# A state-space layer and an attention layer on one core: the kernel's beginning put in a written order, and the work of its first two steps rearranged

## The chip, the cores and the metric

The kernel runs on one core of a Trainium2 chip. The metric is the device time of one execution in microseconds (us). Engines are named as in the profile: PE is the matrix engine (PEld its weight loads), DVE the vector engine, ACT the scalar engine with its function tables, POOL the fourth engine, SP the engine that only issues transfers. ACT and POOL issue transfers too.

## The reference

The input `x` is 4 images (B) of 512 channels (C) and 64 x 64 positions (L = 4096), in float32. Two layers, each with a residual:

```python
x = x + L0(group_norm(x))     # layer norm, mamba on 4 chunks of 128 channels, skip,
                              # layer norm, 512 x 512 projection
x = x + L1(group_norm(x))     # linear attention with 8 heads, ReLU on q and k
```

Group norm has 32 groups of 16 channels and needs the statistics of the whole image. The mamba of layer 0, with 256 inner channels and 16 states, is

```python
xi, z = split(in_proj(x));  xc = silu(conv4(xi) + conv_b)
dt, Bs, Cs = split(x_proj(xc));  dt = softplus(dt_proj(dt) + b)
h = exp(dt * A) * h + (dt * xc) * B_t          # per channel and state, along L
y = sum_over_states(h * C_t) + xc * D_param
out = out_proj(y * silu(z))
```

## The kernel before, in words

An image is cut into 8 tiles of T = 512 positions. A step is one chunk of 128 channels of one tile of one image, so there are 4 x 8 x 4 = 128 steps (`steps`, line 1023). Each step has 16 slots; a slot makes two scans of 128 x 512 on DVE (line 755), where the 128 rows are 32 channels by 4 states.

**What a step needs.** `inputs` (line 593) makes in_proj and convolution together: four products with the shifted tile and the weights `w_cv` give `pc`, a fifth gives `pz`; `silu` (line 1064) follows on ACT. `mixers` (line 658) makes `pd` (x_proj), copies the part for dt to `dt` and sends the rows for B and C to DRAM (`b_rows`, `c_rows`); three bf16 copies and two "minus" products (`parts`) prepare C for the matrix engine. `time_banks` and `time_steps` make dt (`pt`, softplus). `to_rows` (line 640) multiplies dt by xc on POOL and writes both to DRAM (`d_rows`), and `spread` (line 649) reads them back as `d_all`, laid out for the scans: in four parts of two transfers of 256 KB. `b_row` and `c_tail` read B and C back, each row to 32 partitions (`b_all`, `c_sb`).

**A slot** (line 741): `drive` makes `bx` on POOL (line 737) from `d_all` and `b_all`, `decay` makes `dA` with exp on ACT (line 729) into one of three banks, the scan on DVE makes `h`; every second slot `product` (line 775) multiplies `h` by C on DVE, and `fold_states` sums over the states on PE into `y`. Then come gate, out_proj, skip, and for a whole tile `leave`: `layer_scale` (line 461), the projection with `w_pr` (`pp`), the residual, and the store of the tile for layer 1. Norm weights are folded into `w_pr`: it is scaled by `g_sb` (line 315), and its mean over the input channels is taken off (`pw_mean`, line 319, then line 321), the bias goes into `pb` (line 313).

**What sets the order.** The main loop (line 1114) stands under `tc.manual_schedule()`: each engine and queue gets its instructions in an order that follows the written one. Work between slots is put there by hand, by slot numbers, by `later`, and from four queues of generators (`ahead`, `late`, `rest`, `light`) with a credit for PE; the attention of an image runs in these gaps while the next image is in layer 0, and that of the last image after the loop. What stands ahead of the loop, lines 167 to 1112, is left to a scheduler, which may put instructions in another order than the written one. There `now[0]` is `None`, so `later`, `until` and `clear` don't hold anything back. Lines 1201 to 1210, after the loop, have `now[0] = None` too.

**The beginning.** `stats0` (line 810) loads the 8 tiles of image 0 on SP (line 148; three tile buffers, `TILES`) and takes `bn_stats` on DVE (line 816); `aggregate` (line 341) ends it. `stats_end` makes scale and offset per channel. `tile_norm(0, 0)` loads tile 0 again, into `xn` (line 506), applies them on ACT (`group_norm`, line 374), and makes the layer norm: sums over channels on PE, `mu_sums` and `mu`, subtraction on DVE (line 435), squares on ACT (line 443), `var_sums` and `var`, Ln and Exp on ACT, multiplication on DVE (line 421), scale and bias on ACT (line 454). Lines 1091 to 1112 then prepare steps 0 and 1. Meanwhile ACT's queue loads all weights (lines 229 to 285): `w_x`, `conv_bc`, `w_z`, `w_xp` in five pieces, `w_dt`, the columns `dtb`, `dpar`, `g_sb`, `b_sb` (four bytes for each partition and column), `a_sb`, `w_op`, `sk`, `w_pr`, `pb`, `w_qk`, four rows of `b_qk`, `bv`, `bo`. Their preparation stands on DVE: `w_cv` (line 234), `dg` (264), `bqk` (287 to 291), `a_k` (296), the centring of `w_pr`. `a_t` comes from `a_k` with 16 small transfers on SP (line 300).

**Counters of transfers.** In the built program the transfers of SP and ACT share eight completion counters in turn. A transfer waits, before it is issued, for the one eight before it to have landed, whatever queue that one is on.

Of the kernel before, what the change touches and what calls it, by code (L numbers as in the profile page):

```python
# [14 lines left out]
P = 128  # L15
# [9 lines left out]
def kernel(  # L25
# [138 lines left out]
        return load(cols(x, b)[:, :, t * T : (t + 1) * T], f"x{why}_{b}_{t}")  # L164


    ident = wk.tile([P, P], F32, tag="sq", name="ident", bufs=4)
    make_identity(nc, ident)

# [55 lines left out]
    def const_rows(v, name):  # L225
        return rows(v, const.tile([P, v.shape[0] // P, v.shape[1]], F32, tag=name, name=name))
# [4 lines left out]
    nc.scalar.dma_start(w_x, in_w[:, 0:DI])  # L231
    conv_bc = wk.tile([P, NTAP, DI], F32, tag="h", name="conv_bc", bufs=2)
    nc.scalar.dma_start(conv_bc, conv_w.partition_broadcast(P))
    nc.vector.tensor_tensor(w_cv, conv_bc, w_x.unsqueeze(1).to_broadcast([P, NTAP, DI]), ALU.mult)
    w_z = const.tile([P, DI], F32, tag="w_z", name="w_z")
    nc.scalar.dma_start(w_z, in_w[:, DI : 2 * DI])
    cb = column(conv_b, NH, "cb")
# [22 lines left out]
    dpar = column(d_par, NH, "dpar")  # L260

    dg = const.tile([P, NH, BLK], F32, tag="dg", name="dg")
    for e in range(NH):
        nc.vector.tensor_scalar(dg[:, e, :], fold, dpar[:, e : e + 1], None, ALU.mult)
    g_sb = column(norm_g, NC, "g_sb")
    b_sb = column(norm_b, NC, "b_sb")
    skd = const.tile([P, BLK], F32, tag="skd", name="skd")
# [1 line left out]
    w_op = const_rows(op_w, "w_op")  # L269
    sk = const.tile([P, 1], F32, tag="sk", name="sk")  # L270
    nc.scalar.dma_start(sk, skip.partition_broadcast(P))
    w_pr = const_rows(proj_w, "w_pr")
    pb = column(proj_b, NC, "pb")
    w_qk = const_rows(wqk, "w_qk")


    bqk = const.tile([P, C], BF16, tag="bqk", name="bqk")
# [6 lines left out]
    bv = column(b_qkv[2 * C : 3 * C], NC, "bv")  # L284
    bo = column(b_out, NC, "bo")

    nc.vector.tensor_copy(bqk, b_qk)
    for i in (2, 3):
        r = slice(i * LANE, P)
        nc.vector.tensor_tensor(b_qk[r, :], b_qk[r, :], bqk[r, :], ALU.subtract)  # L290
        nc.vector.tensor_copy(bqk[r, :], b_qk[r, :])


    a_k = wk.tile([P, NH, KS, NQ], F32, tag="sq", name="a_k", bufs=4)
    nc.scalar.activation(a_k, a_sb.rearrange("p e (q k) -> p e k q", k=KS), AF.Exp)
    nc.vector.tensor_scalar(a_k, a_k, -1.0, None, ALU.mult)
    a_t = const.tile([P, NH, NJ, NQ], F32, tag="a_t", name="a_t")
    for k in range(KS):
        for j in range(NJ):
            nc.sync.dma_start(  # L300
                a_t[k * BLK : (k + 1) * BLK, :, j, :], a_k[j * BLK : (j + 1) * BLK, :, k, :]
            )
    nc.vector.tensor_scalar(skd, fold, sk, None, ALU.mult)


    for o in range(NC):
        pw = work_bank(f"pw_{o}")
        for c in range(NC):
            mm(
                pw[:, 0:1], w_pr[:, c, o * P : (o + 1) * P], b_sb[:, c : c + 1],  # L310
                start=(c == 0), stop=(c == NC - 1),
            )
        nc.vector.tensor_tensor(pb[:, o : o + 1], pb[:, o : o + 1], pw[:, 0:1], ALU.add)
    for c in range(NC):
        nc.vector.tensor_scalar(w_pr[:, c, :], w_pr[:, c, :], g_sb[:, c : c + 1], None, ALU.mult)

    pw = work_bank("pw_mean")
    for c in range(NC):
        mm(pw, ones.to_broadcast([P, P]), w_pr[:, c, :], start=(c == 0), stop=(c == NC - 1))
    for c in range(NC):  # L320
        nc.vector.scalar_tensor_tensor(
            w_pr[:, c, :], pw, -1.0 / C, w_pr[:, c, :], ALU.mult, ALU.add
        )
    pw = work_bank("pw_about")
    for c in range(NC):
        mm(
            pw[:, 0:1], ones.to_broadcast([P, P]), b_sb[:, c : c + 1],
            start=(c == 0), stop=(c == NC - 1),
        )
    about = const.tile([P, 1], F32, tag="about", name="about")  # L330
    nc.vector.scalar_tensor_tensor(about, pw[:, 0:1], -1.0 / C, sk, ALU.mult, ALU.mult)


    def stats_tile(name):
# [34 lines left out]
    def group_norm(dst, xt, norm):  # L369
        gr, off, _ = norm  # L370
        for c in range(NC):
            if c % 2 == 0:
                yield from clear()
            nc.scalar.activation(
                dst[:, c, :], xt[:, c, :], AF.Identity,
                bias=off[:, c : c + 1], scale=gr[:, c : c + 1],
            )
            if c == 1:
                yield "free"
        yield  # L380
# [12 lines left out]
    def mean_of(sums, what, when, stop=True):  # L393
# [13 lines left out]
        mm(bank, mean.to_broadcast([P, P]), got, start=True, stop=stop)  # L407
        return bank

    def over_deviation(v, var, name):  # L410
        rs = wk.tile([P, T], F32, tag="sq", name=f"rs_{name}", bufs=4)

        def root():
            nc.scalar.activation(rs, var, AF.Ln, bias=eps)
            nc.scalar.activation(var, rs, AF.Exp, scale=-0.5)

        rooted = later(1, root)
        yield
        yield from until(rooted)
        yield "wide"  # L420
        nc.vector.tensor_tensor(v, v, bc(var, NC), ALU.mult)  # L421
        free()
        norming.clear()
        yield

    def layer_norm(v, name):
        while norming:
            yield "wait"
        norming.append(name)
        yield from room()  # L430
        sums = work_bank(f"mu_sums_{name}")
        sums_into(sums, [v[:, c, :] for c in range(NC)], range(NC))
        mu = yield from mean_of(sums, f"mu_{name}", "one ahead")
        yield "wide"
        nc.vector.tensor_tensor(v, v, bc(mu, NC), ALU.subtract)
        free()
        yield "free"
        sqs = []
        for c in range(NC):
            if c % 2 == 0:  # L440
                yield from clear()
            sqs.append(wk.tile([P, T], F32, tag="sq", name=f"sq_{name}_{c}", bufs=4))
            nc.scalar.activation(sqs[c], v[:, c, :], AF.Square)
            if c == 1:
                yield "free"
        yield from room()
        sums = work_bank(f"var_sums_{name}")
        sums_into(sums, sqs, range(NC))
        var = yield from mean_of(sums, f"var_{name}", "two ahead")
        yield from over_deviation(v, var, name)  # L450
        for c in range(NC):
            if c % 2 == 0:
                yield from clear()
            nc.scalar.activation(
                v[:, c, :], v[:, c, :], AF.Identity,
                bias=b_sb[:, c : c + 1], scale=g_sb[:, c : c + 1],
            )
            if c % 2:
                yield "free"
# [43 lines left out]
    def normed(xn, pad, prev_pad, b, t, norm):  # L503

        body = xn[:, :, NTAP - 1 : NTAP - 1 + T]
        nc.sync.dma_start(body, cols(x, b)[:, :, t * T : (t + 1) * T])
        yield from pause(2)
        yield "free"
        if prev_pad is None:
            nc.gpsimd.memset(xn[:, :, 0 : NTAP - 1], 0.0)  # L510
        else:
            nc.gpsimd.tensor_copy(xn[:, :, 0 : NTAP - 1], prev_pad)
        yield from group_norm(body, body, norm)
        yield from layer_norm(body, f"a_{b}_{t}")
        nc.gpsimd.tensor_copy(pad, xn[:, :, T : T + NTAP - 1])
# [130 lines left out]
        f["d_rows", v] = d_rows  # L646
        later(1, lambda: nc.sync.dma_start(d_rows, both[:, v]))

    def spread(f, e, nm, part):

        if part == 0:
            f["d_all", e] = wk.tile([P, 2, NJ, T], F32, tag="d_all", name=f"d_all_{nm}_{e}")
        v, half = divmod(part, 2)
        src = f["d_rows", v].rearrange("(j i) e t -> i e j t", i=BLK)[:, e]
        for k in range(half * KS // 2, (half + 1) * KS // 2):
            nc.sync.dma_start(f["d_all", e][k * BLK : (k + 1) * BLK, v], src)

    def mixers(f, nm):

# [150 lines left out]
    def stats0(stats, b):  # L810

        for t in range(NT):
            xt = yield from load_x(b, t, "s")
            yield
            for c in range(NC):
                nc.vector.bn_stats(stats[:, c, t, :], xt[:, c, :])
                if c == NC - 1:
                    later(1, free_x)
                if c % 2:
                    yield "wait" if c == NC - 1 else None  # L820
# [214 lines left out]
    def input_norm(b):  # L1035
# [2 lines left out]
        norms[b] = yield from stats_end(aggregate(stats, f"a{b}"), f"a{b}")  # L1038
        yield

    def tile_norm(b, t):
        xn[b, t] = wk.tile([P, NC, NTAP - 1 + T], F32, tag="xn", name=f"xn_{b}_{t}", bufs=3)
        pads[b, t] = small.tile([P, NC, NTAP - 1], F32, tag="pad", name=f"pad_{b}_{t}")
        yield from normed(
            xn[b, t], pads[b, t], pads[b, t - 1] if t else None, b, t, norms[b]
        )
# [39 lines left out]
            queue.pop(0)  # L1086
        return False

    run(input_norm(0))
    run(tile_norm(0, 0))  # L1090
    run(step_inputs(0))
    silu(0)
    run(mixers(fs[0], names[0]))
    b_row(0)
    c_tail(0)
    time_banks(fs[0], names[0])
# [1 line left out]
    for v in range(2):  # L1098
        to_rows(fs[0], v, names[0])
    for part in range(4):  # L1100
        spread(fs[0], 0, names[0], part)
    for g in range(JJ, 3 * JJ, JJ):
        b_row(g)
    c_row(0)
    for g in range(2):
        drive(g)
    run(step_inputs(1))
    silu(1)
    run(mixers(fs[1], names[1]))
    nc.scalar.preload_act_table_set("natural_log_exp_and_others")  # L1110
    for k in range(LEAD):
        decay(k)

    with tc.manual_schedule():
        credit, seen, mix, held[0], held_x[0] = 0.0, work["mm"], iter(()), 0, 0
# [148 lines left out]
```

## Time and profile before

| | us |
|---|---|
| median of 3 runs | 7839.31 (7833.92 to 7841.01) |
| the profiled execution, its own time | 7841.1 |
| its span | 7839.4 |
| mean granted clock of PE | 0.905 of full |
| DVE idle in 140 to 7340 | 393.1 of 7200 |
| idle before the first tile's group norm on ACT | 16.34 |
| main loop's first scan starts | 120.77 |
| the last image's attention alone, after the last product (7363.67 + 1.76) | 7365.4 to the end |

The span is the time from first to last instruction in the profile, the execution's own time is 1.7 us longer. Busy times count each engine by itself; a low share is a loss only where no other engine is the bound. The page cuts the span into 40 slices of 196 us, so all of what the change touches at the beginning lies in the first one, and needs the trace's rows.

The early part of the trace, each with its start in us:

| what | start | note |
|---|---|---|
| the loads of the 8 tiles for the statistics, on SP | 0.80, 1.30, 11.96, 13.21, 21.52, 25.23, 35.35, 37.72 | the last lands at 45.2 |
| load of tile 0 into `xn` | 41.79 | |
| subtraction of the mean, L435 | 63.41 | 2.29 long, one 128x2048 |
| `pd` of step 0 | 91.24 | |
| softplus of step 0 | 96.44 and 98.88 | the second ends at 99.57 |
| `d_all` of step 0, 8 transfers | issued 102.92 to 106.6 | 7th landed at 114.5 |
| table load on ACT ahead of the first `dA` | 118.68 | 1.28 long |

### The profile page before, as it was taken

What the parts mean: (1) busy time and instruction counts of PE and PEld (TensorE: products, weight loads), DVE (VectorE), ACT (ScalarE), POOL (GpSimd) and SP (SyncE); (2) the same over time, 40 slices, a digit from 0 to 9 for tenths busy, and PEclk for the clock granted to TensorE, in tenths of its full rate; (3) what the DMA queues carried; (4) which work ended last, traced back from release to release, by engine and by line L of the source; (5) the groups of instructions that cost most, each with busy time, mean ns of one, the idle gap of its engine ahead of it and who ended that gap; (6) DMA issues with size and microseconds to landing.
All of it is one profiled execution on the core that took longest, in us unless ns stands there. A gap on an engine that the chain in (4) does not pass through costs nothing.

```text
span 7839.4 us, 90421 instructions
## 1 busy us (share of the span) xinstructions
PE 6444.4 (82%) x24839; PEld 2099.0 (27%) x24880; DVE 6905.7 (88%) x5650; ACT 5461.7 (70%) x8329; POOL 6898.4 (88%) x4649
## 2 busy tenths in 40 slices
PE   5677777677789888988788888898788888989599
PEld 1121212112223222322222223332222222323144
DVE  5999999999999999999999999999999999999500
ACT  4677777777777777777777777777777777777421
POOL 4999999999999999999999999999999999999500
PEclk7888878888899999998899999999899999999799
DMA  5666666666666656776666666676666666586302
GB/s 164 165 172 168 158 150 162 162 157 169 174 179 169 159 159 159 192 197 169 174 166 169 167 162 160 171 190 183 164 160 168 157 162 154 148 212 182 100 33 91
DMA packets 829184, 1265.87 MB, mean 161 GB/s; under 512 B 183912, under 2 KB 317560, under 8 KB 816384
## 3 DMA queue, kind: packets, MB, share of 16 engines
q1 hardware_dynamic: 804736, 1222.32, 59.6%
q0 software_dynamic: 16896, 33.56, 2.5%
q8 instruction: 195, 3.19, 0.2%
q10 hardware_dynamic: 7040, 4.20, 0.2%
q14 instruction: 317, 2.60, 0.1%
HBM read 1052.78 MB, written 206.57 MB: 161 GB/s over the span
## 4 chain that ended last, share of the span: by engine, by line
DVE 33%; PE 31%; ACT 10%; issue 8%; DMA 7%; POOL 7%; SPq 3%; POOLq 0%; DVEq 0%; ACTq 0%
DVE h L755 21%; DVE h L775 10%; PE pq L129 6%; PE y L129 6%; PE pc L129 5%; POOL bx L737 5%; ACT dA L729 4%; DMA d_all<-d_rows 3%; PE pr L129 3%; PE po L129 2%; SPq L704 2%; PE pp L129 2%; DMA c_sb<-c_rows 2%; PE pd L129 1%; DMA b_all<-b_rows 1%
## 5 line engine op out<-in xcount | busy, mean ns | idle before, releaser
L737 POOL TENSOR_TENSOR bx<-d_all,b_all 128x1024 f32<-128x1024 f32 x2048 | 4824.0, 2367 | 198.2 <-DVE h L755 178.6
L755 DVE TENSOR_TENSOR_SCAN h<-dA,st,bx 128x512 f32<-128x512 f32 x3584 | 4355.5, 1265 | 292.5 <-PE y L129 101.8
L729 ACT ACTIVATE dA<-d_all,a_t 128x512 f32<-128x512 f32 x4096 | 2759.0, 688 | 1491.5 <-DVE h L755 1434.8
L775 DVE TENSOR_TENSOR h<-h,c_all 128x1536 f32<-128x1536 f32 x1024 | 1768.6, 1727 | 0.1
L767 POOL TENSOR_TENSOR h<-h,c_sb 128x512 f32<-128x512 f32 x1024 | 1299.8, 1269 | 99.1 <-DMA c_sb<-c_rows 13.0
L129 PE MATMUL y<-h,fold 128*32 128x512 f32 x8192 | 1264.0, 693 | 45.7 <-POOL h L767 42.4
L129 PE MATMUL c_all<-parts,sel 128*128 128x384 bf16 x1024 | 369.4, 361 | 1021.9 <-DVE h L775 1020.7
L129 PE MATMUL pc<-xn,w_cv 128*128 128x512 f32 x2048 | 1036.6, 639 | 126.0 <-DVE xn L421 62.2
L129 PE MATMUL pq<-w_qk,xa 128*128 128x512 f32 x2048 | 962.5, 602 | 6.7 <-issue 4.1
L755 DVE TENSOR_TENSOR_SCAN h<-dA,bx 128x512 f32<-128x512 f32 x512 | 590.1, 1204 | 76.6 <-ACT dA L729 46.5
L129 PEld LDWEIGHTS pc<-xn,w_cv 128*128 128x128 f32 x2048 | 386.4, 199 | 735.6 <-issue 409.3
L129 PEld LDWEIGHTS <-sel 128*128 128x128 bf16 x1280 | 126.8, 99 | 1668.0 <-DVE h L775 1453.4
L129 PEld LDWEIGHTS pq<-w_qk,xa 128*128 128x128 f32 x2048 | 395.7, 195 | 437.4 <-issue 421.7
L129 PE MATMUL pp<-xn,w_pr 128*128 128x512 f32 x1024 | 478.0, 597 | 3.8 <-DVE xn L421 3.8
L129 PE MATMUL pr<-xb,m 128*128 128x512 f32 x1024 | 476.1, 603 | 4.8 <-POOL m L992 2.2
L129 PE MATMUL y<-xz,dg 32*32 32x512 f32 x2048 | 362.1, 785 | 0.0
L129 PEld LDWEIGHTS y<-h,fold 128*32 128x32 f32 x8192 | 170.5, 114 | 639.7 <-issue 398.1
L848 ACT ACTIVATE kq<-pq 128x512 f32<-128x512 f32 x256 | 150.8, 589 | 265.5 <-PE pq L129 264.8
L797 POOL TENSOR_TENSOR xz<-xz 128x512 f32<-128x512 f32 x256 | 325.1, 1270 | 10.2 <-ACT xz L794 9.3
L644 POOL TENSOR_TENSOR dt<-dt,xz 128x1024 f32<-128x1024 f32 x128 | 302.1, 2360 | 21.4 <-ACT dt L636 21.4
L855 DVE TENSOR_TENSOR kq<-pk,kq 128x256 f32<-128x256 f32 x124 | 51.2, 413 | 277.9 <-PE pk L129 277.7
L129 PE MATMUL pd<-xz,w_xp 128*128 128x512 f32 x512 | 289.3, 692 | 5.2 <-ACT xz L1066 5.2
(178 smaller groups left out, 6164.7 us busy)
## 6 DMA issues: line engine op xcount, KB each, us to landing
d_all<-d_rows SPq DMA_DIRECT2D x2048, 256.0 KB, 4.3
b_all<-b_rows SPq DMA_DIRECT2D x4096, 64.0 KB, 2.3
d_rows<-dt SPq DMA_DIRECT2D x256, 512.0 KB, 2.7
c_sb<-c_rows SPq DMA_DIRECT2D x4096, 16.0 KB, 3.5
xs<-in_x_dram SPq DMA_DIRECT2D x32, 1024.0 KB, 7.8
xn<-in_x_dram SPq DMA_DIRECT2D x32, 1024.0 KB, 8.4
xr<-in_x_dram POOLq DMA_DIRECT2D x32, 1024.0 KB, 10.2
x<-xr SPq DMA_DIRECT2D x32, 1024.0 KB, 4.5
```

The source lines that it names most:

```text
L129: nc.tensor.matmul(out_, lhsT, rhs, **how)
L644: nc.gpsimd.tensor_tensor(f["both"][:, 1], f["both"][:, 0], f["xz"][:, 0], ALU.mult)
L704: nc.sync.dma_start(dst[k * BLK : (k + 1) * BLK, :], rows_[q * KS + k, :].partition_broadcast(BLK))
L729: nc.scalar.activation(dAs[k], fs[n]["d_all", e][:, 0, j, :], AF.Exp, scale=a_t[:, e, j, q : q + 1])
L737: nc.gpsimd.tensor_tensor(bxs[g], fs[n]["d_all", e][:, 1, jj * 2 : jj * 2 + 2, :], bc(b_all[g // JJ], 2), ALU.mult)
L755: nc.vector.tensor_tensor_scan(h[:, j, :], dAs.pop(2 * g + i), bxs[g][:, i, :], 0.0 if t == 0 else st[:, c, e, q, j : j + 1], ALU.mult, AL ...
L767: nc.gpsimd.tensor_tensor(h[:, :, CUT:], h[:, :, CUT:], bc(c_sb.pop(g // JJ), NJ), ALU.mult)
L775: nc.vector.tensor_tensor(own, own, bc(c_all.pop(g // JJ), NJ), ALU.mult)
L797: nc.gpsimd.tensor_tensor(f["xz"][:, 1, e, :], f["xz"][:, 1, e, :], f["xz"][:, 0, e, :], ALU.mult)
L848: nc.scalar.activation(qk[i], pq, AF.Relu)
L855: nc.vector.tensor_tensor(kq, pk, kq, ALU.add)
```

## The change

The whole beginning is put under the manual schedule, so that its order on each engine follows the written one. (1) Tile 0 of `x` is loaded once, first of all, straight into `xn`; its statistics are taken there. (2) `w_pr` and `w_qk` leave ACT's queue: SP loads `w_pr` behind the last tile, `w_qk` behind the 16 transfers of `a_t`. (3) The preparation of the weights on DVE becomes functions called at tiles 2, 4 and 7. (4) Where `now[0]` is `None`, the two DVE operations of a norm (`over`) work in four blocks of 128x512 instead of one 128x2048, and `group_norm` puts chunks 1 and 3 on DVE; this holds after the loop too. (5) `spread` of step 0 comes in 16 transfers of 128 KB, those for the first slots ahead, instead of 8 of 256 KB. (6) The inputs of step 1 stand between the pieces of step 0; its `mixers` come behind the first three `dA`. (7) The offsets `pw`, the scaling and the centring of `w_pr` are spread over the beginning, the centring last; in the built program the four DVE instructions of the centring (line 321 before), though written ahead of the loop, stand between its third and fourth scan. (8) ACT's tables are loaded by written instructions: five before the loop, where there were six. The main loop's own code is unchanged.

```diff
+    front = ExitStack()
+    front.enter_context(tc.manual_schedule())
...
-    w_pr = const_rows(proj_w, "w_pr")
+    w_pr = const.tile([P, NC, C], F32, tag="w_pr", name="w_pr")
     pb = column(proj_b, NC, "pb")
-    w_qk = const_rows(wqk, "w_qk")
+    w_qk = const.tile([P, NC, 2 * C], F32, tag="w_qk", name="w_qk")
...
+    def offset_sums(o):
+        pw[o] = work_bank(f"pw_{o}")
         for c in range(NC):
             mm(
+                pw[o][:, 0:1], w_pr[:, c, o * P : (o + 1) * P], b_sb[:, c : c + 1],
                 start=(c == 0), stop=(c == NC - 1),
             )
...
+    def scaled():
+        for c in range(NC):
+            nc.vector.tensor_scalar(w_pr[:, c, :], w_pr[:, c, :], g_sb[:, c : c + 1], None, ALU.mult)
+
+    def centred():
+        pw = work_bank("pw_mean")
+        for c in range(NC):
+            mm(pw, ones.to_broadcast([P, P]), w_pr[:, c, :], start=(c == 0), stop=(c == NC - 1))
+        for c in range(NC):
+            nc.vector.scalar_tensor_tensor(
+                w_pr[:, c, :], pw, -1.0 / C, w_pr[:, c, :], ALU.mult, ALU.add
+            )
...
+            if now[0] is None and c % 2:
+                nc.vector.tensor_scalar(
+                    dst[:, c, :], xt[:, c, :], gr[:, c : c + 1], off[:, c : c + 1], ALU.mult, ALU.add
+                )
+            else:
+                nc.scalar.activation(
...
+    def over(v, m, op):
+
+        if now[0] is None:
+            for c in range(NC):
+                nc.vector.tensor_tensor(v[:, c, :], v[:, c, :], m, op)
+        else:
+            nc.vector.tensor_tensor(v, v, bc(m, NC), op)
...
-    def spread(f, e, nm, part):
+    def spread(f, e, nm, part, by_slot=False):
...
+        if by_slot:
+            half, v = divmod(part, 2)
+            ks, js = range(KS), slice(half * NJ // 2, (half + 1) * NJ // 2)
...
     def stats0(stats, b):
 
         for t in range(NT):
+            if (b, t) in xn:
+                for c in range(NC):
+                    nc.vector.bn_stats(stats[:, c, t, :], xn[b, t][:, c, NTAP - 1 :])
+                continue
             xt = yield from load_x(b, t, "s")
-            yield
+            yield t if now[0] is None else None
...
-    run(input_norm(0))
-    run(tile_norm(0, 0))
+    nc.scalar.preload_act_table_set("natural_log_exp_and_others")
+    new_xn(0, 0)
+    nc.sync.dma_start(xn[0, 0][:, :, NTAP - 1 :], cols(x, 0)[:, :, 0:T])
+    for t in input_norm(0):
+        if t == 2:
+            prepare_conv()
+        elif t == 4:
+            prepare_d()
+            prepare_bias()
+        elif t == NT - 1:
+            nc.sync.dma_start(w_pr, proj_w.rearrange("(c p) f -> p c f", p=P))
+            prepare_a()
+            nc.sync.dma_start(w_qk, wqk.rearrange("(c p) f -> p c f", p=P))
+    wide, taking = 0, []
+    for what in tile_norm(0, 0):
+        for o in taking:
+            offset_take(o)
+        taking = []
+        if what == "wide":
+            taking = ([0], [1, 2])[wide]
+            wide += 1
+            for o in taking:
+                offset_sums(o)
+    nc.scalar.preload_act_table_set("silu_and_others")
     run(step_inputs(0))
     silu(0)
-    run(mixers(fs[0], names[0]))
+    nc.scalar.preload_act_table_set("softplus")
+    second = step_inputs(1)
+    for _ in range(2):
+        next(second)
+    first = mixers(fs[0], names[0])
+    next(first)
+    next(first)
+    next(second)
     b_row(0)
     c_tail(0)
     time_banks(fs[0], names[0])
...
     for part in range(4):
-        spread(fs[0], 0, names[0], part)
+        spread(fs[0], 0, names[0], part, True)
+    nc.scalar.preload_act_table_set("silu_and_others")
+    run(second)
+    run(first)
+    c_row(0)
+    silu(1)
+    nc.scalar.preload_act_table_set("natural_log_exp_and_others")
     for g in range(JJ, 3 * JJ, JJ):
         b_row(g)
-    c_row(0)
     for g in range(2):
         drive(g)
-    run(step_inputs(1))
-    silu(1)
-    run(mixers(fs[1], names[1]))
-    nc.scalar.preload_act_table_set("natural_log_exp_and_others")
     for k in range(LEAD):
         decay(k)
+    offset_sums(3)
+    offset_take(3)
+    scaled()
+    run(mixers(fs[1], names[1]))
+    centred()
+    front.close()
```

## The prediction

> **What bounds the kernel now.** I read the page first, by engine and by slice.
>
> ```profile
> PE 6444.4 (82%) x24839; PEld 2099.0 (27%) x24880; DVE 6905.7 (88%) x5650; ACT 5461.7 (70%) x8329; POOL 6898.4 (88%) x4649
> DVE  5999999999999999999999999999999999999500
> ```
>
> Between a weak first slice and a weak end VectorE is above nine tenths in every slice. The windows view tells where the first slice is lost:
>
> ```profile
> 60.00:80.00 20.00, 11.03 (x21) 2.76 (x17) 4.58 (x2) 7.57 (x12) 0.19 (x1) 0.59 0.00 0
> 100.00:110.00 10.00, 9.97 (x21) 3.92 (x19) 0.00 (x0) 2.67 (x5) 1.98 (x1) 0.86 0.82 229
> 120.00:140.00 20.00, 11.85 (x37) 3.02 (x37) 18.08 (x15) 14.28 (x20) 18.99 (x13) 0.57 0.83 218
> 140.00:160.00 20.00, 13.55 (x59) 3.68 (x57) 20.00 (x17) 16.93 (x25) 19.76 (x14) 1.00 0.78 216
> ```
>
> Columns: window, length, busy time of PE, weight load, DVE, ACT, POOL, then clock, DMA share, GB/s. From 120 us DVE is the bound (1.92 us idle in 120–140, none in 140–200); before, the front is a chain. The main loop's order is the same in both builds on every engine, so a shift of the first product (L775) should reach the end unchanged. So I price the front up to that product, then the tail. The front's chain stands in the timeline:
>
> ```profile
> 51.78 1.04 DVE L341 BATCH_NORM_AGGREGATE mv_a<-st 128x2 f32<-128x48 f32 x4
> 56.68 2.93 ACT L374 ACTIVATE xn<-xn,off_a,gr_a 128x512 f32<-128x512 f32 x4 [16.34 <-DMA a_t<-a_k]
> 74.03 2.29 DVE L421 TENSOR_TENSOR xn<-xn,var_a 128x2048 f32<-128x2048 f32 x1 [8.33 <-ACT var_a L415]
> 77.22 9.70 PE L129 MATMUL pc<-xn,w_cv 128*128 128x512 f32 x16 [4.58 <-ACT xn L454]
> 99.59 2.77 SPq L647 DMA_DIRECT2D d_rows<-dt  x2
> 115.83 6.95 POOL L737 TENSOR_TENSOR bx<-d_all,b_all 128x1024 f32<-128x1024 f32 x3 [13.85 <-DMA b_all<-b_rows]
> 120.77 5.68 DVE L755 TENSOR_TENSOR_SCAN h<-dA,bx 128x512 f32<-128x512 f32 x5 [44.45 <-ACT dA L729]
> 126.37 1.73 DVE L775 TENSOR_TENSOR h<-h,c_all 128x1536 f32<-128x1536 f32 x1
> ```
>
> Start, busy time, engine, line; brackets hold the idle time and its releaser. The statistics end (S) at 52.82 (51.78 + 1.04), `pc` starts at 77.22, the first `bx` at 115.83, the first product at 126.37. I work out these four stretches: 52.82, 24.40, 38.61, 10.54.
>
> **1. Statistics: 52.82 → 42.0.** In SP's waits the tile loads are held by buffers and by other transfers:
>
> ```profile
> SPq L148 <- DVE st L816: 16.3, 4, 9.7
> SPq L148 <- DMA w_xp<-in_xp_w_dram: 10.1, 1, 10.1
> ```
>
> (Total, count, longest.) A load waits for the transfer eight earlier on its queue's counters. The change starts four tiles at once instead of three (with the weights some 5 MB at the 363 GB/s of window 5–10: the fourth lands at about 17.7), but puts new links in front of the rest. In the built order `dtb`'s issue on ACT waits for tile 3; `dpar`, `g_sb`, `b_sb`, `a_sb` follow, about 0.35 us each. `b_sb` is issued at about 19.5, and tile 5's load waits for it. The trace shows such column loads landing 4.8 to 9.0 us after issue (`dpar` 6.7, `b_sb` 9.0, both under six competing loads); I take 5.3, since only one tile then moves: 24.8. Tile 6 waits for `pb` in the same way, a little later. `b_qk`'s third and fourth rows wait for `a_sb` and tile 4 in the same way; the last lands at about 28; its five casts (0.41 + 0.69 + 0.42 + 0.69 + 0.42 = 2.63 by their rows) now stand on DVE ahead of tile 4's `bn_stats`, queued behind them: 30.7. Tile 4 takes 2.46 (the row of four 128x512): 33.1. That releases tile 7's load, which lands 4.8 later (5 to 7 have come): 38. Tiles 5 and 6 fill DVE to 38.1, `a_k` and `skd` 0.4, tile 7 2.46, L341 1.04: 42.0. Ends: 39 (casts ready early) and 46 (columns at 9.0). **−10.8.** Moved to SP behind tile 7, `w_pr` lands at about 40 and `w_qk` at about 55; `w_pr` is first read after the mean's "wide" block, at about 52, `w_qk` in the attention: cost nothing, with over 10 us of cover, and each us beyond it would cost one.
>
> **2. Norm: 24.40 → 21.1.** Two engines for L374: last block at +1.51 (two of .73) instead of +2.93: −1.4. [...] The row of L421 is 2.29 for 2048 columns; 512 columns take 0.69 alone, with a pitch of .615 in a row (2.46 for four): 2.54. [...] by the row +.25. At the mean the squares on ACT start after the first block (.69, not 2.29) and follow block by block: −1.3. At the deviation `pc` waits, in the built order, for all four blocks and for ACT's L454 of the first, which now runs beside them: 2.54 instead of 2.29 + .87, −0.6 [...]. **−3.3** (ends −2 and −4.2).
>
> **3. `pc` to `bx`: 38.61 → 32.8.** Removed: an ACT table load from the path (1.3, as in 118.68's 1.28). Added: `pd` of step 0 stands behind step 1's `pc_0_1_0` on PE, 8 x .43 = 3.44, of which 2.1 lies on the path (the rest is under silu). Softplus of step 0 then ends at +21.9 (before +22.35), the two `d_rows` issue at +22.6 and +24.4, and the second lands at +27.2 (2.8, the row of 102.01). `d_all` comes in 16 loads of 128 KB, first slots' halves first: at the 205 GB/s seen here `bx_0` needs 1 MB instead of 2, 5.1 instead of 10.2 us. From +27.2 (the second half's last source) that puts its last part at about +32.6 and `bx_0` at +32.8: **−5.8** (ends −3, if SP, which took .53 for each of the eight issues at 102.92 to 106.6, paces the loads, and −7). `dA_0` is ready at +30.8. Before, it was the later one (scan at 120.77, table load before it), so `bx_0` becomes the limit.
>
> **4. `bx` to first product: 10.54 → 17.4.** This is the part that I had not expected from the diff. In the built order the four centring instructions of `w_pr` (before: 39.52, idle DVE, hidden) stand on DVE between the third scan and the fourth, though written ahead of the loop:
>
> ```profile
> 33.59 5.90 PE L129 MATMUL pw_mean<-w_pr,ones 128*128 128x512 f32 x8 [0.65 <-DVE w_pr L315]
> 39.52 2.48 DVE L321 SCALAR_TENSOR_TENSOR w_pr<-pw_mean,w_pr 128x512 f32<-128x512 f32 x4 [1.23 <-PE pw_mean L129]
> ```
>
> They wait for `pw_mean`, which stands on PE behind the second "minus" product of step 1, which waits for an ACT copy, which stands behind `dA_3` and `dA_4`, which wait for scans 0 and 1. Behind the waiting DVE instruction: scans 3 and 4 and the product; they hold `dA_5`ff on ACT, `bx_3` on POOL (buffer) and the first fold on PE. Scan 1 ends at T = +4.8 from the start of `bx_0` (2.35 for it, 2.45 for two scans). `pw_mean` starts T + 1.7 (`dA`, copy, matmul), ends T + 7.6, the centring T + 10.2, two scans 2.4: product at T + 12.6 = +17.4: **+6.9.** [...] by the row 5.90 (five at .85). I take the row. Ends: 0 (`pw_mean` done in time, if PE is warm and the copy early) and +8. The other pieces put there (`scaled` 4 x .42, `pw_3`, L325) lie in the wait for `bx_0`: nothing, with some 8 us of cover.
>
> **5. Tail.** The last layer's deviation comes in four blocks: `pp` starts after .69 instead of 2.30 (chain: L421 at 7387.09, `pp` at 7389.43): −1.6 (ends 0 and −2). The last group norm on two engines: PE is 49.5 of 50 us busy there: 0.
>
> **Sum.** −10.8 − 3.3 − 5.8 + 6.9 − 1.6 = −14.6. The profiled execution took 7841.1 (span 7839.4), so 7826.5; it lies 1.8 above the median 7839.3, so the median becomes **7824.7**. The first product should be at about 113.4. A measurement can tell about 0.2%, 15.7 us, from no change: 7823.6 and below is faster, and the forecast lies just inside "same".
>
> **The rivals.** A (0.55) is this sum, between −11 and −19 as its terms miss by a few us; as 15.7 lies just beyond its middle, .23 of it is faster by over 0.2%.
> B (0.27): the centring hardly holds DVE, because PE comes to it early and warm. For it: nothing but the ACT copy stands before it[...]; against it: `dA_3`, ahead of that copy, needs the bank that scan 0 frees. Then the +6.9 shrinks to between +1.5 and 0: −20.0 to −21.5, 7818 to 7819, faster.
> C (0.15): the columns take their 9.0, S at 46 as above: −10.8 becomes −6.8: −10.6, 7828.7, same. For it: `b_sb` itself took 9.0; against it: six loads ran beside it.
> D (0.03): the same link, grown: tile 5 is held by `b_sb`, ordered behind `dtb`'s wait. Each us that `b_sb` lands beyond 24.8 costs one us; from 24.8 + 14.6 = 39.4 on the kernel is slower than before, and by over 0.2% from 55.1 (at 56: 7824.7 + 31.2 = 7855.9). Against it: no column load took over 9.0.
> That the shift doesn't reach the end (E, within A and C): DVE idles 393 of the 7200 us after 140, and where it waits there for a transfer that isn't later in step, the gain could shrink. But the loads' issues stand in the same written order and shift along, and the median of three runs that spread by 7.1 us decides no finer. If half were lost, −7: 7832, same.
>
> **How the numbers follow.** All favourable ends give −13.8 − 4.2 − 7 + 0 − 2 = −27: 7812, the low end, where B with its own favourable ends stops. All unfavourable give −6.8 − 2 − 3 + 8 = −3.8; C with one of them, or half the shift lost, is at about −6 to −7: 7834 with some spread. About 2 in 10 lie outside. Faster .23 + .27 = .50; same .32 + .15 = .47; slower .03.
>
> **What would show it.** L341's end at 42 (39: casts early; 46: C); `pc` 21.1 later; the first `bx` 32.8 after that, on half the loads; a DVE gap of about 7 us before the centring's stt, released by PE `pw_mean`; the first product at 113.4; 140–200 without DVE idle time. I am wrong if the product comes before 108 (B), or if the end doesn't follow it (E).

## The result and the profile after

The changed kernel took 7820.14 us in the median of 10 runs (7810.72 to 7829.56), the kernel before, beside it, 7840.16: ratio 0.9974, 95% interval 0.9964 to 0.9983, that is −20 us (−28 to −13). Run again later (first experiment) the ratio was 0.9982 (0.9975 to 0.9988), −14 us (the two medians differ by 13.1). The profiled execution took 7826.28 (span 7824.6), 14.8 less than that of before; 14.6 were forecast. The page's first rows:

```profile
PE 6445.2 (82%) x24880; PEld 2100.6 (27%) x24880; DVE 6914.7 (88%) x5677; ACT 5447.9 (70%) x8310; POOL 6898.0 (88%) x4649
DVE  6999999999999999999999999999999999999500
```

The busy times are those of before within 14 us; only the first slice is fuller. The windows show where (columns as before):

```profile
60.00:80.00 20.00, 19.19 (x46) 10.14 (x45) 2.61 (x6) 10.71 (x13) 0.19 (x1) 1.00 0.00 0
100.00:110.00 10.00, 6.25 (x12) 2.72 (x12) 3.56 (x3) 4.49 (x8) 7.52 (x4) 0.58 0.66 155
120.00:140.00 20.00, 19.12 (x65) 5.91 (x61) 18.94 (x16) 16.50 (x25) 19.57 (x15) 0.86 0.68 197
140.00:160.00 20.00, 11.99 (x52) 2.68 (x50) 19.89 (x16) 16.27 (x24) 19.73 (x14) 0.91 0.62 140
```

From 120 us on DVE is as full as before. The clock column needs care: the clock records of this trace begin only at 70.9 us, and the view counts what lies ahead of them as 1.00, though the passes there took twice the time of the later ones (0.85 and 0.43 us). The front's chain in the timeline, with the same columns as in the prediction:

```profile
42.21 1.04 DVE L359 BATCH_NORM_AGGREGATE mv_a<-st 128x2 f32<-128x48 f32 x4
47.10 1.52 ACT L397 ACTIVATE xn<-xn,off_a,gr_a 128x512 f32<-128x512 f32 x2 [18.46 <-POOL xn L542]
...
62.67 2.48 DVE L437 TENSOR_TENSOR xn<-xn,var_a 128x512 f32<-128x512 f32 x4 [6.70 <-ACT var_a L446]
...
65.30 9.87 PE L129 MATMUL pc<-xn,w_cv 128*128 128x512 f32 x16 [0.81 <-DVE pb L327]
...
98.24 2.34 POOL L773 TENSOR_TENSOR bx<-d_all,b_all 128x1024 f32<-128x1024 f32 x1 [8.38 <-DMA d_all<-d_rows]
...
100.61 2.34 DVE L791 TENSOR_TENSOR_SCAN h<-dA,bx 128x512 f32<-128x512 f32 x2 [5.45 <-POOL bx L773]
...
104.50 5.55 PE L129 MATMUL pw_mean<-w_pr,ones 128*128 128x512 f32 x8
...
110.09 2.48 DVE L340 SCALAR_TENSOR_TENSOR w_pr<-pw_mean,w_pr 128x512 f32<-128x512 f32 x4 [3.74 <-PE pw_mean L129]
...
114.80 1.73 DVE L811 TENSOR_TENSOR h<-h,c_all 128x1536 f32<-128x1536 f32 x1
```

The bracket of the centring (L340) is the new wait: DVE stands 3.74 us behind the third scan, until `pw_mean` is there. Ahead of the third scan, at 105.12, it had waited 2.18 us for POOL's `bx`. And SP's waits for the tiles' loads (total, count, longest):

```profile
SPq L148 <- DMA w_xp<-in_xp_w_dram: 14.6, 1, 14.6
SPq L148 <- DVE st L856: 8.3, 1, 8.3
SPq L148 <- DMA sk<-in_skip_dram: 6.3, 1, 6.3
```

The loads now wait 8.3 us for a buffer and, in two waits, 20.9 us for other transfers' landing. (The view puts the last wait down to `sk`; by the counter that this load uses it is `b_sb`, which landed at 24.94, and the load was issued at 24.99.) The stretches:

| us | before | forecast | after | again |
|---|---|---|---|---|
| statistics end | 52.82 | 42.0 | 43.25 | 43.60 |
| from there to `pc` | 24.40 | 21.1 | 22.05 | 22.05 |
| `pc` to first `bx` | 38.61 | 32.8 | 32.94 | 33.58 |
| `bx` to first product | 10.54 | 17.4 | 16.56 | 15.84 |
| first product starts | 126.37 | 113.4 | 114.80 | 115.07 |
| first product's start to last product's end | 7239.06 | as before | 7239.26 | 7238.54 |
| tail behind it | 473.96 | 472.4 | 470.53 | 470.56 |

### The profile page after: what moved, and what is told of

Its sections match the earlier page's. It is cut to its first block, busy times and chain, and to the rows that moved or that the text cites. A ratio compares the mean times of both kernels' runs of the same rounds, so it can differ in the third digit from the quotient of the medians.

```text
span 7824.6 us, 90512 instructions
## 1 busy us (share of the span) xinstructions
PE 6445.2 (82%) x24880; PEld 2100.6 (27%) x24880; DVE 6914.7 (88%) x5677; ACT 5447.9 (70%) x8310; POOL 6898.0 (88%) x4649
## 4 chain that ended last, share of the span: by engine, by line
DVE 35%; PE 30%; ACT 11%; DMA 8%; issue 8%; POOL 6%; SPq 3%; DVEq 0%; POOLq 0%; ACTq 0%
DVE h L791 22%; DVE h L811 10%; PE y L129 6%; PE pc L129 6%; PE pq L129 6%; POOL bx L773 4%; ACT dA L765 4%; DMA d_all<-d_rows 3%; PE pr L129 3%; PE po L129 2%; PE pp L129 2%; DMA c_sb<-c_rows 2%; SPq L740 2%; DVE xn L439 2%; PE c_all L129 1%
## 5 line engine op out<-in xcount | busy, mean ns | idle before, releaser
L791 DVE TENSOR_TENSOR_SCAN h<-dA,bx 128x512 f32<-128x512 f32 x512 | 590.0, 1202 | 40.7 <-POOL bx L773 17.7
```

The source lines that it names most:

```text
L791: nc.vector.tensor_tensor_scan(h[:, j, :], dAs.pop(2 * g + i), bxs[g][:, i, :], 0.0 if t == 0 else st[:, c, e, q, j : j + 1], ALU.mult, AL ...
```

## The experiments

Each is an edit of the changed kernel. Where a median is compared with the kernel before, the latter ran beside it. Experiments 5 to 8 and 10 are one profiled execution each; the others have a profile and a median of 6 to 21 runs.

**1. The changed kernel again.** No edit.

> The changed kernel once more, unaltered, beside the three variants, to see how far a span wanders from one execution to the next. Theory (the gain is the shift of the first product, 11.6 us, plus the tail, 3.4 us, carried one to one): the front repeats within 0.3 us (statistics end at 43.2, first product at 114.8), the tail repeats at 470.5 us behind the last product, and whatever differs in the span lies between the first and the last product; against the kernel before about -15 us. Rival (the main loop itself became faster by some 5 us, which would make the measured median difference of 20): the stretch from first to last product is shorter than in the kernel before in this execution too, by about 5 us, and the ratio is at 0.9974 again.

Measured: the two last columns above; 7825.57 against 7838.71, ratio 0.9982 (0.9975 to 0.9988). The rival falls: the loop took 7239.26 and 7238.54 us, before 7239.06. On the way through the loop the shift against the profile of before wanders between −2.0 and −16.0 (in the other execution −9.8 to −18.0) and ends at −11.4 and −11.8. The interval of the first medians, −28 to −13, holds the 14.8 of the profiles; what goes beyond it is taken for scatter (each kernel's runs spread over some 15 us and more), and no cause for it was seen.

**2. The centring out of the first scans' way.**

```diff
-            taking = ([0], [1, 2])[wide]
+            taking = ([0], [1, 2, 3])[wide]
...
+    scaled()
     nc.scalar.preload_act_table_set("silu_and_others")
...
     run(second)
-    run(first)
-    c_row(0)
     silu(1)
     nc.scalar.preload_act_table_set("natural_log_exp_and_others")
+    centred()
+    run(first)
+    c_row(0)
...
-    offset_sums(3)
-    offset_take(3)
-    scaled()
     run(mixers(fs[1], names[1]))
-    centred()
```

> Only the folding of the norm into w_pr is placed otherwise: the fourth offset and the scaling right behind the first norm, the centring (pw_mean and its four VectorE operations) ahead of the first scans, behind the inputs of step 1. The output is the same. Theory (6.0 us of the first stretch are the centring's wait between third and fourth scan): first bx stays at 98 to 98.6, first product at 108.5 to 109.5, that is 10.4 to 11 behind bx instead of 16.6, no VectorE gap released by pw_mean; the total is 5 to 6 us below the changed kernel's, about -20 against before in a pair of profiles, ratio about 0.9968. Rival (scans 3 and 4 would have waited anyway for their dA, bx or for c_all, so that the hold is covered): the product stays later than 112.

Measured: `bx` at 99.36 and product at 109.82, both a little past their ranges, 10.46 apart; median 7825.29, that of experiment 1 within 0.3. A median with an interval of some 5 us on either side can't tell a gain of 2 from none. DVE in the timeline of this kernel:

```profile
101.74 2.34 DVE L791 TENSOR_TENSOR_SCAN h<-dA,bx 128x512 f32<-128x512 f32 x2 [3.32 <-POOL bx L773]
106.38 3.52 DVE L791 TENSOR_TENSOR_SCAN h<-dA,bx 128x512 f32<-128x512 f32 x3 [2.30 <-POOL bx L773]
109.82 1.73 DVE L811 TENSOR_TENSOR h<-h,c_all 128x1536 f32<-128x1536 f32 x1
...
130.14 1.22 DVE L791 TENSOR_TENSOR_SCAN h<-dA,bx 128x512 f32<-128x512 f32 x1 [1.25 <-POOL bx L773]
```

The hold was worth its price at the first product (5.3 less than in the repeated run), and the half of the expectation that took it for carried fell: the later brackets name POOL. At the seventh product only 2.1 of the 5.3 are left (shift −13.91 against −11.78). POOL began its chain of `bx` no earlier than in experiment 1 (99.36 and 99.23), so it is late next. At the last product the shift was −9.6, and this profile's tail took 474.44.

**3. The casts of `bqk` behind the norm.** `prepare_bias()` is called after the first norm instead of at tile 4.

> The five casts of bqk on VectorE are written behind the first norm instead of ahead of the fifth tile's statistics; they are read only in the attention. Theory (the casts' wait for the last row of b_qk, at 29.16, holds the fifth tile's bn_stats, which landed at about 25.4, and with it the load of the eighth tile): fifth tile's bn_stats at 25.4, eighth tile issued at 27.9 to 28.5 instead of 34.46, statistics end at 39.5 to 40.5 instead of 43.25, first product about 3 earlier. Rival (the column loads set the pace: tiles six and seven are issued only after b_sb and pb have landed): statistics end later than 42, the gain under 1.3.

```profile
23.75 2.47 DVE L856 BATCH_NORM_STATS2 st<-xs 128x6 f32<-128x512 f32 x4
...
38.68 1.04 DVE L359 BATCH_NORM_AGGREGATE mv_a<-st 128x2 f32<-128x48 f32 x4
```

The fifth tile's statistics start at 23.75 instead of 31.96, and they all end at 39.72: −3.5, as the theory has it. First product at 108.43, shift at the seventh −18.2; median 7823.03, ratio 0.9979 (0.9970 to 0.9987). Against experiment 1 the first product came 6.6 earlier; 1.4 of this have another cause: from the statistics to `pc` 20.67 instead of 22.05 with the same instructions. At the last product the shift was −14.6. PE in the timeline of the changed kernel and of this one:

```profile
59.21 2.07 PE L129 MATMUL var_a<-got_var_a,mean 128*128 128x512 f32 x2 [0.68 <-ACT got_var_a L421]
```

```profile
55.25 1.12 PE L129 MATMUL var_a<-got_var_a,mean 128*128 128x512 f32 x2 [0.68 <-ACT got_var_a L421]
```

Two passes in 1.12 instead of 2.07: PE was at full clock one time and at half the other. The clock records agree: the first rise lies at 54.0 here and at 70.9 in the changed kernel.

**4. PE kept busy in the tail.**

```diff
-        if now[0] is None:
+        if now[0] is None and not late:
...
         yield "wide"
+        if now[0] is None and late:
+            spare = work_bank("spare", 0)
+            for i in range(3):
+                mm(spare, ones.to_broadcast([P, P]), rs, start=(i == 0), stop=(i == 2))
         over(v, var, ALU.mult)
```

> In the tail alone the last deviation is one 128x2048 operation again, and three matmuls of 128x512 whose result nothing reads are put on PE ahead of the projection, fed by the logarithm's output so that they fall into the gap in which PE waits. The front is unchanged. Theory (of the tail's 3.4 us 1.6 are the earlier start of the projection and 1.7 its clock: PE idle for 3.79 us ahead of it made the first passes slow, idle for 2.19 us does not): the projection starts 24.0 behind the last product as in before, but takes 14.0, not 15.7; tail 472.0 to 472.3. Rival (the 1.7 us come from the blocks: the projection's later products don't wait, or from the group norm on two engines): the projection takes 15.7 with a warm PE too, tail 473.8.

The projection in the profiles of before, of after and of this kernel:

```profile
7389.43 15.70 PE L129 MATMUL pp<-xn,w_pr 128*128 128x512 f32 x32 [3.79 <-DVE xn L421]
```

```profile
7376.46 14.00 PE L129 MATMUL pp<-xn,w_pr 128*128 128x512 f32 x32 [2.19 <-DVE xn L437]
```

```profile
7374.64 2.84 PE L129 MATMUL spare<-rs_b,ones 128*128 128x512 f32 x6 [0.84 <-ACT rs_b L445]
7377.68 13.98 PE L129 MATMUL pp<-xn,w_pr 128*128 128x512 f32 x32 [0.20 <-DVE xn L439]
```

It starts 24.09 behind the last product, as before, and takes 13.98: with the gap filled the 1.7 us are gone though the norm is one operation. Tail 471.79 (0.2 below the expected range), median 7826.73. The theory holds for this pair of gaps; the last section has two executions in which the projection was slow though the gap was 2.19.

**5. `d_all` in 256 KB again.** `spread(fs[0], 0, names[0], part)` without the last argument.

> The changed kernel, with d_all of step 0 spread as before: 8 transfers of 256 KB, no order by slots. Theory (the first bx waits for 1 MB instead of 2): first bx 12.9 us behind the first issue as in the kernel before, instead of 7.0, so at 102.5 to 104.1 instead of 98.2; the fifth bx operand later no worse; first product 4 to 6 later, at 119 to 121. Rival (SP's issuing of 16 transfers costs what the halves gain): first bx within 1 us of 98.2.

The first `bx` comes at 104.09, 5.85 later, as expected; the first product at 116.70, only 1.9 later. DVE shows why:

```profile
108.64 2.48 DVE L340 SCALAR_TENSOR_TENSOR w_pr<-pw_mean,w_pr 128x512 f32<-128x512 f32 x4 [13.19 <-PE pw_mean L129]
...
111.11 5.67 DVE L791 TENSOR_TENSOR_SCAN h<-dA,bx 128x512 f32<-128x512 f32 x5
```

So the edit moved two things: in this build the centring stands ahead of all scans. Most of DVE's 13.19 us is a wait that it would have had for `bx` anyway; the first scan starts 4.7 behind the end of that `bx`, and with all of `d_all` there no scan waits again, so that the product comes 12.61 behind the first `bx` instead of 16.56. Of the 5.85 that the order by slots gives to `bx`, 1.9 reach the product as the changed kernel stands, or 2.6 counted from `pc`, which this execution reached 0.7 earlier, PE's clock being up (21.10).

**6. Step 1's inputs behind step 0's spread.** The three `next(second)` are left out, and `run(second)` does it all.

> The changed kernel, with the inputs of step 1 written behind the spread of step 0 in one piece, so that pd of step 0 no longer stands behind step 1's eight passes of pc. Theory (2.1 of the 3.4 us of these passes lie on step 0's path): from pc to first bx 30.8 to 31.5 instead of 32.9; but silu of step 1 then ends at about 97 and the first dA, behind it on ACT, comes at 98 to 99, so that the first product gains at most 1. Rival (the passes lie wholly under the two silu operations): pc to bx within 0.5 of 32.9.

From `pc` to `bx` 30.69, 0.1 below the expected range. `pd` here, and in the changed kernel:

```profile
75.77 1.98 PE L129 MATMUL pd<-xz,w_xp 128*128 128x512 f32 x4 [1.33 <-ACT xz L1110]
```

```profile
80.16 1.88 PE L129 MATMUL pd<-xz,w_xp 128*128 128x512 f32 x4
```

Here PE waits for ACT's silu (its `xz`, which ended at 75.72); there PE came straight from step 1's passes, 2.0 after that silu had ended at 78.16. The first product came at 111.22: −3.6, where at most −1 was expected. 1.1 of it is PE's clock ahead of `pc` (20.91); the first `dA` came at 94.42, not at 98 to 99, and `bx` stayed the limit.

**7. `w_pr` and `w_qk` on ACT's queue again.** Both by `const_rows` in their old places, the two loads on SP left out.

> The changed kernel, with w_pr and w_qk loaded where the kernel before had them, on ACT's queue ahead of pb and of b_qk. Theory (most of the 9.6 us of the statistics come from these 3 MB no longer standing among the tiles: 3 MB at some 360 GB/s are 8.7): statistics end at 49 to 53 instead of 43.3. Rival (they come from loading tile 0 once): statistics end within 2 of 43.3.

Statistics end at 53.30, 10.05 later, first product at 125.38; the other stretches of the front are those of after within 1.2.

```profile
39.27 0.43 DVE L297 CAST bqk<-b_qk 128x512 bf16<-128x512 f32 x1 [15.46 <-DMA b_qk<-in_b_qkv_dram]
```

This is what the 3 MB do: `b_qk` stands behind them, and DVE waits 15.46 us for it instead of 4.96, with the fifth tile's statistics behind the cast. What they would cost without the casts in that place (experiment 3) was not run.

**8. Tile 0 loaded twice.** `new_xn(0, 0)` and its load stand behind tile 7's load instead of first.

> The changed kernel, with tile 0 loaded twice as before: once for the statistics, and once more into xn, behind tile 7 and ahead of w_pr on SP. Theory (the tile buffers are not what holds the loads, the counters and the transfers ahead are; the second load lands under the small operations after the statistics): statistics end within 1 of 43.3, group norm starts within 1 of 47.1, first product at 114 to 116. Rival (one tile more is 1 MB, 2.9 to 5 us on the path): statistics or group norm 3 to 5 later, first product at 118 to 120.

Statistics end at 41.10, 2.15 earlier than after, which neither the theory nor the rival had; first product at 112.56. Loading once gives nothing to the time and even costs these 2.15: with three tiles started at once instead of four, `dtb`'s turn comes at 13.11 instead of 17.91, and with it the columns, `b_sb` at 15.71 instead of 19.39.

**9. A longer front.** In `stats0` the eighth tile's four `bn_stats` are made eight times.

> The changed kernel, with the eighth tile's bn_stats made eight times instead of once (the same four instructions again, with the same result), so that VectorE ends the statistics 7 x 2.4 to 2.5 = 17.2 us later. Theory (a shift of the front is carried to the end one to one): statistics end at 60.4, first product 17.2 later at 132, and the median 17.2 above the changed kernel's, ratio to before 1.0002 to 1.0006. Rival (the loop lies on something that doesn't shift along, so that part of a shift is lost or given back): the median rises by less than 12 or by more than 22.

Statistics end at 59.57 (+16.3); the first product at 129.18 (+14.4; 0.9 of the difference is PE's clock, which was up ahead of `pc`, 21.11). The median is 7841.85, ratio to before 1.0002 (0.9994 to 1.0010): 16.3 above that of experiment 1, or 15.7 by the ratios, within some 8 us. Within this interval a shift of the front is carried one to one. The profiled execution, at 7850.56 one of the longer, doesn't show it: its loop took 7249.02, 10 more than that of before.

**10. Norms in one piece.** `over` always takes the 128x2048 form, `group_norm` ACT alone.

> The changed kernel, with both operations of a norm as one 128x2048 again and the group norm on ACT alone, in the front and in the tail. Theory: from the statistics to pc 24.4 as in before instead of 22.05 (2.4 to 3.3 of the norm's stretch are these edits); tail 474.0 or 470.5 plus 1.6, as PE's clock falls, instead of 470.5. Rival (the clock, not the blocks, makes the front's difference): statistics to pc 22 to 23.

From the statistics to `pc` 24.24, tail 474.03: both are those of before, within 0.2. PE had full clock in this front from `var_a` on (1.12), half clock there in that of before and of after (2.07 both). So the edits are worth 24.24 less 20.67 to 21.11 where both had full clock (experiments 3, 6, 9), that is 3.1 to 3.6. The 24.40 less 22.05, 2.35, also holds 0.96 of clock against the change: `mu_a` took 1.12 in before and 2.08 in after. In the tail they are worth 3.5 with start and clock.

**11. Two edits together** (experiments 3 and 6).

> Two of the single edits together: the casts of bqk behind the norm, and the inputs of step 1 behind step 0's spread. Theory (both add up): statistics end at 39.7, pc at 60.4 to 61.8, first bx at 91 to 92.6, first product at 107.6 to 109.2, 6 to 7 earlier than in the changed kernel; median 4 to 7 below the changed kernel's, ratio to before 0.9973 to 0.9977. Rival (beyond some 13 us the first steps are limited by POOL and by transfers that don't come earlier, as when the centring was moved): the shift has shrunk by 2 or more at the seventh product, and the median lies within 3 of the changed kernel's.

Statistics at 39.66, `bx` at 93.17, product at 110.48, later than expected: the hold grew to 17.31 as `bx` came earlier. Median 7822.22, ratio 0.9975 (0.9965 to 0.9985). The shift at the seventh product, −15.3, is 3.5 more than in experiment 1: the edits add up only in part, and the hold takes the rest.

**12. And the centring ahead.** As 11, with `scaled()` behind the first norm, as in experiment 2, and

```diff
     silu(0)
+    centred()
     nc.scalar.preload_act_table_set("softplus")
```

> As the kernel with both edits, and the centring of w_pr moved ahead: fourth offset and scaling right behind the first norm, pw_mean behind the silu of step 0, where PE waits for ACT. Theory: pw_mean costs PE's path 1 to 2, statistics to pc +0.7; first bx at 93 to 95, no VectorE gap released by pw_mean, first product 10.4 to 12.7 behind it, at 104 to 107; of the gain of 6 some 2 to 3 are carried beyond the seventh product, POOL being next; median 2 to 4 below the kernel with both edits. Rival (nothing beyond both edits is carried): median within 1.5 of that kernel's.

```profile
77.03 2.49 DVE L340 SCALAR_TENSOR_TENSOR w_pr<-pw_mean,w_pr 128x512 f32<-128x512 f32 x4 [10.67 <-PE pw_mean L129]
...
105.62 1.73 DVE L811 TENSOR_TENSOR h<-h,c_all 128x1536 f32<-128x1536 f32 x1
```

The centring lies in DVE's idle time, `bx` at 95.18 pays 2.0 for it, and the first product is 10.44 behind. At the seventh product the shift is −19.6, 4.3 more than in 11; 1.8 of these are PE's clock (from the statistics to `pc` 21.85, in experiment 2 with the same pieces 23.69). Median 7815.95 against 7841.59, ratio 0.9969 (0.9958 to 0.9981): the lowest of all kernels here, though its interval meets the changed kernel's.

## Why the prediction was right, step by step

**Statistics: 43.25, forecast 42.0.** The links came as named: `dtb` issued at 17.91 (about 17.7 forecast), `b_sb` landed at 24.94 (24.8), the casts begun at 29.16 (28.1 by the sum). Two were mis-sized: `b_qk`'s last row, issued at 25.40, let the cast start 1.1 later than that, and tile 7 came 0.41 after DVE was free for it, where the sum had it there before. (The columns' issues lie 0.44 to 0.52 apart, not 0.35; the forecast's 19.5 for `b_sb`, measured 19.39, fits the former.) The forecast left open which of the edits gives the gain: it is the 3 MB taken off ACT's queue (10.05, experiment 7), while the single load of tile 0 gives nothing (8), and the casts on DVE still hold back 3.5 (3). The 10.05 hold for the order with the casts on DVE.

**Norm: 22.05, forecast 21.1.** The three terms came as forecast: −1.4 at the group norm, −1.4 at the mean, −0.6 at the deviation. For four blocks against one the trace has 2.48 against 2.29, +0.19: near the row's +0.25, and less than four single blocks of 0.69 would add (2.76, +0.47). What was mis-sized is PE's own work, taken as the same on both sides: the two passes of `mu_a`, which the subtraction waits for, ran at full clock before and at half clock after, +0.96. Before and after:

```profile
62.25 1.12 PE L129 MATMUL mu_a<-got_mu_a,mean 128*128 128x512 f32 x2 [0.67 <-ACT got_mu_a L398]
```

```profile
51.31 2.08 PE L129 MATMUL mu_a<-got_mu_a,mean 128*128 128x512 f32 x2 [0.71 <-ACT got_mu_a L421]
```

The small `pw` passes, new in this place, end at 64.49, ahead of the fourth block (65.15), and hold nothing back.

**`pc` to `bx`: 32.94, forecast 32.8.** Two misses cancel: the first `d_all` was issued at +25.9, earlier than allowed for, and the first MB took 7.0 from there. The softplus at +21.9 doesn't follow from the two terms that are named for it, −1.3 and +2.1, which give +23.15; measured it was +22.14, as `pt` took 1.12 instead of 2.07. The price of the eight passes ahead of `pd` was 2.1 in the sum; taking them away gave 2.25 (6).

**`bx` to product: 16.56, forecast 17.4.** The wait is where it was put, with the causes in their order (`pw_mean` 104.50, centring 110.09), though the gap ahead of the centring was 3.74 and not about 7: the third scan had waited 2.18 of it for `bx`. `pw_mean` took 5.55, 0.35 less than the row's 5.90: its first five passes began 0.85 us apart, the last three 0.43, and the clock rose at 108.42. That PE would be warm by then (0.43 us a pass), as B has it, was the author's estimate. The rival B was wrongly sized: with the hold gone and the first `bx` at the same time, 2.1 are carried to the seventh product, not 5.4 to 6.9 (2), because POOL's `bx` and the second half of `d_all` are late next. Experiment 12 agrees: of its 4.3, 2.5 are left without PE's clock. The prediction asked what is late next for its own sum, not for that rival.

**Tail: −3.43, forecast −1.6.** The projection starts 1.60 earlier, as worked out. The other 1.7 were overlooked: PE's idle time ahead of it fell from 3.79 to 2.19 and its first passes kept full clock (4). In experiments 2 and 8 the clock fell (15.70 us for the projection) though the gap was 2.19, so that the gap's length alone doesn't decide; the last section shows what else it went with. The group norm on two engines gave nothing, as forecast: behind the projection's end the tail took 434.26 before and 434.13 after. (The 49.5 of 50 us were read from a later window; in 7400 to 7450, where that norm stands, PE was busy for 30.87 of 50.)

**The loop** carried the shift: −11.57 at the first product, −11.37 at the last in the profile, and some +16 in the median for +16.3 at the statistics' end and +14.4 at the first product (9). Single executions are less faithful: in the 13 profiles of the changed kernel and its variants the loop took 7238.5 to 7249.5, so that the end came up to 10.4 later than the first product promised (10.0 in 9, 10.4 in 5, whose tail of 464.86 gave 5.7 back, 6.9 in 2, 2.9 to 4.0 in 3, 6 and 7). What sets this is open; that part of a shift is lost, the prediction's E, is ruled out only for the medians, within their intervals.

In sum the front missed by +1.4 and the tail by −1.8, so that −14.6 met −14.8 in part by two errors of opposite sign. The medians alone would have misled: −20 is the number of B, whose mechanism the trace rules out, and just beyond A's −19; the repeat's −14 lies within A. Which way they differ from −14.8 is scatter of runs as far as these runs can tell.

## What to carry to other kernels

Price a moved instruction by what waits behind it on its engine at the new place: four operations that cost nothing in idle time took 6 us between two scans. When you take such a wait away, ask what is late next before you count its length: here POOL and a transfer kept 3 of 5 us. Big weight loads that nothing needs soon should stand behind small ones that a busy engine waits for: that alone was 10 us in this order, while saving a whole load of 1 MB was nothing.

## What the runs showed of the hardware that had not been expected

The same PE instructions, at the same place in the program, ran at full clock in some executions and at half in others: the two passes of `var_a` took 1.12 or 2.07 us. Experiments 5 and 6 change nothing ahead of `pc`, and yet from the statistics to `pc` they took 21.10 and 20.91 us instead of 22.05; over all variants with the same instructions there it was 20.67 to 22.90 (experiments 3 and 8). So PE's clock moves the first product by 1 to 2 us with nothing changed ahead of it.

The clock records of the traces tell more. In the traces of before and after (406 and 404 records) all changes of the clock lie whole multiples of 3.41 us apart, within 0.05 us, and this grid does not start with the program: its first point would lie 0.49 us into the span in before and 2.61 in after. In after the next point of the grid came 0.32 us behind the statistics' end (43.57), and `var_a` ran at half clock; in experiment 3, with the same instructions from the statistics to `var_a`, the rise at 54.0 puts the next point some 0.6 us behind the statistics' end, and `var_a` ran at full clock.

In before the clock fell at 7390.34, 0.91 us into the projection, at the end of an interval of the grid in which PE had been busy for only 0.87 of 3.40 us. In after PE was busy for 1.98 us in the interval from 7372.0 and for 2.34 in the next, and the clock stayed. The interval that holds most of the gap, in before, after and experiment 2:

```profile
7386.90:7390.30 3.40, 0.87 (x2) 0.49 (x3) 2.29 (x1) 0.15 (x1) 0.00 (x0) 1.00 0.00 0
7375.40:7378.80 3.40, 2.34 (x6) 1.14 (x7) 2.48 (x4) 0.28 (x1) 0.00 (x0) 1.00 0.00 0
7377.80:7381.20 3.40, 1.22 (x3) 0.67 (x4) 1.96 (x4) 1.29 (x2) 0.00 (x0) 1.00 0.00 0
```

In experiments 2 and 8 the gap of 2.19 us lay whole in one interval, and the projection took 15.70 us with the blocks in place (tail 474.4); in after a point of the grid, 7375.4, cut it in two. So the 1.7 us of the tail went, in these traces, with where the gap fell in the grid. Three matmuls without use in the gap kept the clock up, 13.98 instead of 15.70 us for 32 passes (4). An interval with PE busy for 1.22 us went with a fall (experiment 2), one with 1.98 with none (after); what lies between, and what makes the clock rise, these runs do not show.
